# Splitting one block product of each Strassen-like weight product once more, on one core of a Trainium2 chip

## The chip, the cores and the metric

The kernel runs on one NeuronCore of a Trainium2 chip. The metric is the device time of one execution in microseconds (us); less is better. The engines are named as the profile names them: PE is TensorE (PEld its weight loads), DVE is VectorE, ACT is ScalarE, POOL is GpSimd, and SP is SyncE, whose queue starts nearly all of the DMAs.

## The reference, cut to what matters

The input x holds 128 graphs of 128 nodes with 512 features, in float32. Four layers follow one another; each ends with `x = layernorm(x + layer(x))` over the features.

```python
# layer 0
y = einsum('nm,bmd->bnd', adj, x);  out = y @ weight + bias
# layer 1
q, k, v = x @ Wq.T, x @ Wk.T, x @ Wv.T
rel = adjacency.T * (q @ k.T);  rel = rel / norm(rel, axis=2);  out = rel @ v
# layer 2
h = x @ W;  e = leaky_relu(h @ a1 [:, None] + h @ a2 [None, :]) * mask
out = elu(softmax(e) @ h + beta * h)
# layer 3 (W1 = W2 = adj, so C - A is b)
A = einsum('od,bdn->bon', adj, x);  out = max over n of relu(A + b)   # one number per node
```

All products stay in float32. The costly ones are products of a (512 x 512) activation block with a 512 x 512 weight; there are four of them for each set of four graphs.

## The kernel before, in words

**Groups.** The 128 graphs are taken in 32 groups of G = 4, so that a group is a matrix of 512 rows (4 graphs x 128 nodes) by 512 features. Each group passes through `layer0` to `layer3`.

**The four products of a group.** They are called y (weight "0", layer 0), m (weight "m" = Wq and Wk multiplied ahead, layer 1), v (weight "v", layer 1) and z (weight "2", layer 2). Each is a 512 x 512 x 512 product in 2 x 2 blocks of 256, taken in seven block products in place of eight (the scheme of Strassen and Winograd). The sums of the weight's blocks are made once (`weight_blocks`, on DVE). The sums of the left blocks are made for each group on POOL (`left_factors`, four additions of 128x512 for y, for z, and for x, which m and v share; they are the tiles s_y, s_z and s_x). A block product is four matmuls of 128 x 128 weights with 256 columns.

**Where the sums lie.** `product` issues the block products in `ORDER = (1, 2, 6, 5, 7, 3, 4)`. `REGION` says in which PSUM bank each accumulates: 1, 6, 7 and 4 go into one bank (tag r0, which has two buffers), 2 into the bank r12, and 5 and 3 into a later use of r12, which has one buffer. The sums in a bank are used while they grow: after product 1 the bank is read out to output block (0, 0), then product 6 is added on top and the bank is read out to block (0, 1), and so on. So every block product after the first in a bank waits until the read-out before it is done. For m, v and z the first write of an output block (after 1, 6, 5 and 4) is a copy by ACT, and the others are additions by DVE (`out` in `product`). For y all are additions by DVE on top of x, and the two banks are filled with the bias by ACT beforehand (`fill`).

**Order.** Nothing is ordered by data alone. Every operation is emitted with a place in time (`emit(at, f)`), all are sorted by it, and `InOrder` keeps that order on each engine. A place is counted in steps of one block product; a group takes 28 steps, and its four products stand at steps 0 (m), 7 (y of the next group), 14 (v) and 21 (z) of a round. Between the block products stand the other matmuls: `aggregate` (p_y, four matmuls of 128 columns per graph) between those of m, `scores` (p_rel) between those of y, `gather` (p_z) between those of v, and `widen` (p_a) and `attend` (p_o), one matmul of 512 columns per graph, between those of z. Their places are in `TABLE`; the first and last groups have their own in `FIRST` and `LAST`.

**Banks.** PSUM has r0 (2 banks), r12 (1), wa (2) and `bank()` (tag ps, 3), which p_y, p_rel, p_z, p_a and p_o take in turn.

**What stands around the products.** ACT copies p_y to yT and p_z to zT, takes the exponentials (of c into a tile that is also called m, and of e) and the second halves of the layer norms (x from x, nmean, rstd). DVE has the other read-outs, the statistics, `elu` (x from c, x from the exponential m, then the statistics), `dots` (scr from x and wa) and the softmax around `weighted`, which is a POOL multiplication (e from e and adj). `greatest` (nm from e) on DVE waits for it.

Of the kernel before, what the change touches and what calls it, by code (L numbers as in the profile page):

```python
# [8 lines left out]
FP = mybir.dt.float32  # L9
# [20 lines left out]
def kernel(  # L30
# [52 lines left out]
    dram = ctx.enter_context(tc.tile_pool(name="dram", bufs=2, space=bass.MemoryType.DRAM))  # L83

    def bank(name):
        return psum.tile([P, D], FP, tag="ps", name=name, bufs=3)

    def on_all(row, n):

# [27 lines left out]

    w2_sb = const.tile([P, K, D], FP)
    nc.sync.dma_start(w2_sb, w2.rearrange("(k p) f -> p k f", p=P))
    a_sb = data.tile([P, 2, D], FP, tag="x3", name="a_sb")  # L120
    nc.sync.dma_start(a_sb.rearrange("p s d -> p (s d)"), on_all(a2, 2 * D))
    beta_sb = const.tile([P, 1], FP)
    nc.sync.dma_start(beta_sb, on_all(beta, 1))
# [33 lines left out]
    def weight_blocks(at, key, w, keep=0, tag=None):  # L157

        def blk(kh, ch):
            return w[:, 2 * kh : 2 * kh + 2, H * ch : H * ch + H]

        t = {}

        def factor(i):
            if i == 0:
                home, args = (const, {}) if tag is None else (data, dict(tag=tag))
                u = home.tile([P, 3 + keep, 2, H], FP, name=f"t_{key}", **args)
                t.update({2: u[:, 0], 3: u[:, 1], 4: u[:, 2]})  # L170
                t[1] = u[:, 3] if keep else blk(0, 1)
                bw[key] = {
                    1: blk(0, 0), 2: blk(1, 0), 3: blk(1, 1), 4: t[4], 5: t[1], 6: t[2], 7: t[3],
                }
            to, left, op, right = (
                (3, blk(1, 1), ALU.subtract, blk(0, 1)),
                (2, t[3], ALU.add, blk(0, 0)),
                (4, blk(1, 0), ALU.subtract, t[2]),
                (1, blk(0, 1), ALU.subtract, blk(0, 0)),
            )[i]  # L180
            dve.tensor_tensor(t[to], left, right, op)

        for i in range(4):
            emit(at[i], factor, i)

    bw = {}


    def prepare_v(c):
# [7 lines left out]
    def prepare_dots(k):  # L197

        for i in range(2):
            scr = work.tile([P, D], FP, tag="scr", name=f"scr_wa_{i}_{k}", bufs=2)  # L200
            dve.scalar_tensor_tensor(
                scr,
                w2_sb[:, k, :],
                1.0,
                a_sb[:, i, :],
                op0=ALU.mult,
                op1=ALU.mult,
                accum_out=col[:, i, k : k + 1],
            )
# [14 lines left out]
    def emit(at, f, *args):  # L224
        pieces.append((at, lambda: f(*args)))
# [5 lines left out]
    def row(at, step, n=G):  # L231
# [4 lines left out]
        load=[-20], y=row(0.5, 1), y_sums=row(4.3, 0.5), y_w=row(7, 1, 7),  # L236
        stats0=row(14.4, 0.4), norm0=[16.2], apply0=row(16.8, 0.33),
        turn=row(21.4, 1), turn_blocks=row(18.4, 0.6),
        move=row(20.5, 0.1), x_sums=row(25.3, 0.5), m=row(28, 1, 7), scores=row(36.5, 1),
        masked=[39.95], squares=[40.4], turn_rel=[40.3],  # L240
        move_rel=row(41.2, 0.1), inverse=[42.5], v=row(42, 1, 7), attend=row(50.6, 1),
        residual=row(51.0, 1), dots=[51.7, 53.8, 54.9, 55.6], norm1=[54.6], scale=[57.2],
        apply1=row(65.4, 0.33),
        spread=[57.3], leaky=[62.6], weighted=[62.9], greatest=[63.9], exps=[64.0],
        divide=[65.2], turn_att=[68.6], with_beta=[69.0], turn_blocks_2=[65.7], move_2=[65.8], gather=row(71.5, 1),
        z_sums=row(75.3, 0.5), z_w=row(77, 1, 7), exp=[86.0, 87.0, 96.0, 99.6],
        elu=[86.4, 87.4, 96.8, 100.3], norm2=[101.4], apply2=row(102.4, 0.33),
        widen=[104.2, 104.9, 105.6, 106.3], top=[104.7, 105.4, 106.1, 106.8],
# [53 lines left out]
    REGION = {1: 0, 6: 0, 7: 0, 4: 0, 2: 1, 5: 2, 3: 2}  # L302
    BLOCK = {1: (0, 0), 2: (0, 0), 6: (0, 1), 3: (0, 1), 5: (1, 1), 7: (1, 1), 4: (1, 0)}

    def left_factors(at, s, aT, tag, name, keep):
# [14 lines left out]
        emit(at[1], lambda: pool.tensor_tensor(s["f"][6], s["f"][5], blk(0, 0), ALU.subtract))  # L320
        emit(at[2], lambda: pool.tensor_tensor(s["f"][7], blk(0, 0), blk(1, 0), ALU.subtract))
        emit(at[3], lambda: pool.tensor_tensor(s["f"][3], blk(0, 1), s["f"][6], ALU.subtract))

    def by_rows(p, a, b, first):

# [21 lines left out]
                    skip_group_check=True,  # L347
                )

    def product(at, name, mul, s, w, c, fresh, begin=None, before=None, lead=0.7):  # L350
# [29 lines left out]
        def out(i):  # L380
            p, dst = r[REGION[i]], c(*BLOCK[i])
            if fresh and i in (1, 6, 5, 4):
                act.copy(dst, p)
            else:
                dve.tensor_tensor(dst, p, dst, ALU.add)

        for n, i in enumerate(ORDER):
            if before is not None and i in (1, 5):
                emit(at[n] - (0.7 if i == 5 else lead), fill, REGION[i])
            emit(at[n], step, i)  # L390
            emit(at[n] + 0.72, out, i)
# [46 lines left out]
    def layer0(g, t):  # L438
        s = {}

        def aggregate(b):
# [12 lines left out]
                s["yT"][:, :, b * P : (b + 1) * P], p.rearrange("p (k n) -> p k n", k=K)  # L454
            )

        if g > 0:
            emit(t["load"][0], load, g)
        each(t["y"], aggregate)
        left_factors(t["y_sums"], s, "yT", "s_yz", f"y_{g}", 0)  # L460
        product(
            t["y_w"],
            f"y_{g}",
# [4 lines left out]
            False,  # L468
            before=bias_halves,
            lead=4.4 if g == 0 else 0.7,  # L470
        )
        each(t["stats0"], lambda b: stats(s, f"0_{g}", b, x1[g][:, b, :]))
        norm(t["norm0"], t["apply0"], s, f"0_{g}", lambda: x1[g])
# [2 lines left out]
    def layer1(g, t):  # L476
# [128 lines left out]
        def dots(b):  # L605
            if b == 0:
                s["d"] = small.tile([P, 2, G], FP, tag="d12", name=f"d12_{g}")
            for i in range(2):
                scr = work.tile([P, D], FP, tag="scr", name=f"scr_{g}_{b}_{i}", bufs=2)
# [27 lines left out]
        else:  # L637
            each(t["turn_blocks"], turn_blocks)
            each(t["move"], move)
        left_factors(t["x_sums"], s, "xT", "s_x", f"x_{g}", 1)  # L640
        product(t["m"], f"m_{g}", by_columns, s, "m", middle_block, True, begin_middle)
        each(t["scores"], scores)
        emit(t["masked"][0], masked)
        emit(t["squares"][0], squares)
# [3 lines left out]
        else:  # L648
            emit(t["turn_rel"][0], turn_last)
        emit(t["inverse"][0], inverse)  # L650
        product(t["v"], f"v_{g}", by_rows, s, "v", rows_of(lambda: s["v"]), True, begin_values)
        each(t["attend"], attend)
        each(t["residual"], residual)
        if g == NG - 1:
# [10 lines left out]
    def layer2(g, t):  # L665
# [66 lines left out]
            engine.tensor_tensor(e, e, rs[:, :, None].to_broadcast([P, n, P]), ALU.mult)  # L732

        def turn_att(i):
            if i == 0:
                s["p"] = bank(f"p_eT_{g}")
            for b in range(i * n, i * n + n):
                pe.transpose(s["p"][:, b * P : (b + 1) * P], s["e"][:, b, :], ident)

        def with_beta(i):  # L740
            if i == 0:
                s["eT"] = work.tile([P, G, P], FP, tag="eT", name=f"eT_{g}")
            dve.tensor_tensor(
                s["eT"][:, i * n : i * n + n, :],
                s["p"].rearrange("p (b n) -> p b n", b=G)[:, i * n : i * n + n, :],
                beta_b[:, i * n : i * n + n, :],
                ALU.add,
            )
# [57 lines left out]

        def elu(b):
            if b == 0:
                if g < NG - 1:
                    x3[g] = data.tile([P, G, D], FP, tag="x3", name=f"x3_{g}")  # L810
# [21 lines left out]
            emit(t["move_2"][0], move)  # L832
        each(t["gather"], gather)
        if g < NG - 1:
            left_factors(t["z_sums"], s, "zT", "s_yz", f"z_{g}", 0)
            product(t["z_w"], f"z_{g}", by_rows, s, "2", rows_of(lambda: s["c"]), True, begin)
        else:
            each(t["z_w"], direct)
        each(t["exp"], exp)
# [5 lines left out]
    def layer3(g, t):  # L845
        s = {}

        def widen(b):
            s["a", b] = bank(f"p_a_{g}_{b}")
            pe.matmul(s["a", b], adjT, x3[g][:, b, :], start=True, stop=True)  # L850


# [153 lines left out]
```

## Time and profile before

| What | Value |
|---|---|
| Median of 3 runs | 2173.91 us (2173.57 to 2174.77) |
| The profiled execution's own time | 2173.83 us |
| Its span in the profile | 2172.0 us |
| PE matmul busy | 2149.1 us, 99% |
| DVE busy | 1560.6 us, 72% |
| ACT busy | 1115.4 us, 51% |
| POOL busy | 720.8 us, 33% |
| Mean granted PE clock | 0.996 |

The span is the time from the first to the last instruction that the profile shows; the execution's own time has 1.83 us more around it. A matmul in float32 appears as two records. Busy shares are means over the whole span, and matmuls overlap in the records, so the distance from the start of one group of records to the start of the next is the better measure of what a matmul costs PE.

### The profile page before, as it was taken

The numbers are of one execution on the slowest core, as the hardware profiler recorded it, in microseconds if no ns is written. First come the engines' busy times: TensorE is split into PE (matmuls) and PEld (weight loads), VectorE is DVE, ScalarE is ACT, GpSimd is POOL, SyncE is SP. The second block draws the span as 40 slices with busy tenths as digits, with TensorE's granted clock in tenths as the row PEclk, the third lists the DMA queues.
The fourth block names the chain that finished last, engine by engine and source line by source line (L and its number), as shares of the span: only waits on it lengthen the run. The fifth ranks groups of instructions, "written<-read, shape, count | busy, mean of one in ns | idle before, by whom it ended". The sixth has DMA issues, their size and how long they took to land.

```text
span 2172.0 us, 31973 instructions
## 1 busy us (share of the span) xinstructions
PE 2149.1 (99%) x10887; PEld 1820.3 (84%) x10887; DVE 1560.6 (72%) x3429; ACT 1115.4 (51%) x2470; POOL 720.8 (33%) x589
## 2 busy tenths in 40 slices
PE   9999999999999999999999999999999999999996
PEld 8888888888888888888888888888888888888882
DVE  4667676776777776777777767767777767777677
ACT  3235545555545555455555455554455554555554
POOL 4223333333333233334233233323332333333331
PEclk9999999999999999999999999999999999999998
DMA  4012222322122322222222223222322222332201
GB/s 171 25 37 64 58 72 72 71 54 59 59 76 66 77 55 51 67 73 69 55 58 62 74 71 73 54 56 62 75 67 66 58 56 70 74 68 55 39 20 59
DMA packets 361970, 138.31 MB, mean 64 GB/s; under 512 B 303184, under 2 KB 318672, under 8 KB 361808
## 3 DMA queue, kind: packets, MB, share of 16 engines
q1 hardware_dynamic: 361280, 135.22, 24.8%
q8 instruction: 88, 1.44, 0.3%
q10 hardware_dynamic: 528, 1.05, 0.1%
q14 instruction: 74, 0.61, 0.1%
HBM read 55.12 MB, written 41.48 MB: 44 GB/s over the span
## 4 chain that ended last, share of the span: by engine, by line
PE 97%; DVE 2%; ACT 0%; POOL 0%; issue 0%; ACTq 0%; POOLq 0%; DVEq 0%
PE r_m L26 18%; PE r_y L26 18%; PE r_v L26 18%; PE r_z L26 17%; PE p_rel L26 5%; PE p_y L26 5%; PE p_o L26 5%; PE p_z L26 5%; PE p_a L26 5%; PE r_qk L26 1%; DVE st L26 1%; DVE x L26 0%; DVE mx L26 0%; PE first_r L26 0%; ACT x L26 0%; PE c L26 0%
## 5 line engine op out<-in xcount | busy, mean ns | idle before, releaser
L26 ACT ACTIVATE x<-x,nmean,rstd 128x512 f32<-128x512 f32 x384 | 285.4, 807 | 48.6 <-DVE nmean L26 45.1
L26 DVE BATCH_NORM_STATS2 st<-x 128x6 f32<-128x512 f32 x392 | 268.3, 685 | 9.7 <-ACT x L26 1.1
L26 POOL TENSOR_TENSOR rstd<-ve,mhalf 128x4 f32<-128x4 f32 (+1 forms) x99 | 109.3, 1104 | 340.3 <-DVE ve L26 340.3
L26 DVE TENSOR_TENSOR x<-r_y,x 128x512 f32<-128x512 f32 x224 | 152.4, 680 | 91.7 <-PE r_y L26 83.7
L26 ACT COPY yT<-p_y 128x512 f32<-128x512 f32 x128 | 74.9, 586 | 195.6 <-PE p_y L26 195.6
L26 DVE SCALAR_TENSOR_TENSOR scr<-x,wa 128x512 f32<-128x512 f32 x256 | 162.0, 679 | 0.0
L26 DVE TENSOR_REDUCE mx<-p_a 128x1 f32<-128x512 f32 x128 | 88.3, 690 | 99.6 <-PE p_a L26 96.8
L26 ACT ACTIVATE x<-x,mean,r 128x512 f32<-128x512 f32 x128 | 97.4, 808 | 113.9 <-DVE mean L26 112.4
L26 POOL TENSOR_TENSOR rn<-n,mhalf 128x4 f32<-128x4 f32 x32 | 32.6, 1017 | 358.3 <-ACT sq L26 358.3
L26 PEld LDWEIGHTS p_z<-eT,x 128*128 128x128 f32 x1024 | 133.8, 192 | 8.0 <-issue 0.9
L26 PEld LDWEIGHTS p_rel<-xT,tT 128*128 128x128 f32 x1024 | 134.0, 192 | 6.7 <-ACT tT L26 0.2
L26 PEld LDWEIGHTS p_y<-adjT,x 128*128 128x128 f32 x1024 | 133.6, 192 | 6.3
L26 ACT COPY tT<-r_m 128x512 f32<-128x512 f32 x128 | 75.6, 590 | 119.1 <-PE r_m L26 119.1
L26 DVE TENSOR_TENSOR tT<-r_m,tT 128x512 f32<-128x512 f32 x96 | 66.3, 691 | 96.9 <-PE r_m L26 94.2
L26 PE MATMUL p_rel<-xT,tT 128*128 128x128 f32 x1024 | 134.7, 275 | 0.0
L26 PE MATMUL p_z<-eT,x 128*128 128x128 f32 x1024 | 134.5, 275 | 0.1
L26 PE MATMUL p_y<-adjT,x 128*128 128x128 f32 x1024 | 134.1, 275 | 0.0
L26 POOL TENSOR_TENSOR s_y<-yT 128x512 f32<-128x512 f32 x32 | 40.6, 1269 | 281.1 <-ACT yT L26 281.1
L26 PE MATMUL p_a<-x,adjT 128*128 128x512 f32 x256 | 128.7, 606 | 5.1 <-ACT x L26 5.1
L26 ACT COPY zT<-p_z 128x512 f32<-128x512 f32 x128 | 73.7, 576 | 116.5 <-PE p_z L26 116.5
L26 PE MATMUL p_o<-v,relT 128*128 128x512 f32 x256 | 129.7, 592 | 0.0
L26 ACT COPY v<-r_v 128x512 f32<-128x512 f32 x128 | 74.2, 580 | 107.9 <-PE r_v L26 107.9
(157 smaller groups left out, 5218.7 us busy)
## 6 DMA issues: line engine op xcount, KB each, us to landing
out_dram<-x SPq DMA_DIRECT2D x128, 256.0 KB, 2.1
x<-in_x_dram SPq DMA_DIRECT2D x31, 1024.0 KB, 7.6
xT<-xB SPq DMA_DIRECT2D x480, 64.0 KB, 2.3
relT<-relB SPq DMA_DIRECT2D x496, 16.0 KB, 1.8
eBd<-eB SPq DMA_DIRECT2D x30, 256.0 KB, 2.0
eT<-eBd SPq DMA_DIRECT2D x120, 64.0 KB, 2.0
s<-s2d SPq DMA_DIRECT2D x29, 256.0 KB, 5.2
w_sb<-in_L_gnn_weight_dram ACTq DMA_DIRECT2D x1, 1024.0 KB, 6.0
```

The source lines that it names most:

```text
L26: return lambda *args, **kw: self.tc.keep_in_program_order(op(*args, **kw))
```

## The change

One of the seven block products of 256, number 2, is itself taken in seven products of blocks of 128, in place of its four matmuls with 256 columns. It therefore has seven matmuls with 128 columns. Its sums lie in a PSUM bank of their own (tag pi), which is taken from `bank()`: ps has two buffers in place of three. The seven small sums are read out by seven DVE additions of 128x128 onto output block (0, 0), where there was one of 128x512. The left sums of the small product are four POOL additions of 128x128 at the end of `left_factors` (`inner_sums`), and those of the weight are made once on DVE.

The order of a product with a small one inside is `WITH_SMALL`: 1, 6, 5, 7, 3, 4, with the small matmuls in four pieces between them (`SMALL`). `scores` and `gather` stand one step earlier. y of groups 2 to 31, m and v of groups 1 to 30 and z of groups 0 to 29 are taken so: 30 of each, 120 products. Some tiles have fewer buffers (scr, x3, a_sb), and in the last groups some transposes and `widen` use the banks pi and r12.

```diff
     def bank(name):
-        return psum.tile([P, D], FP, tag="ps", name=name, bufs=3)
+        return psum.tile([P, D], FP, tag="ps", name=name, bufs=2)
...
-        move=row(20.5, 0.1), x_sums=row(25.3, 0.5), m=row(28, 1, 7), scores=row(36.5, 1),
+        move=row(20.5, 0.1), x_sums=row(25.3, 0.5), m=row(28, 1, 7), scores=row(35.5, 1),
...
-        divide=[65.2], turn_att=[68.6], with_beta=[69.0], turn_blocks_2=[65.7], move_2=[65.8], gather=row(71.5, 1),
+        divide=[65.2], turn_att=[68.6], with_beta=[69.0], turn_blocks_2=[65.7], move_2=[65.8], gather=row(70.5, 1),
...
+        def inner_sums():
+            a = {
+                (j, k): s[aT][:, 2 + k, j * P : (j + 1) * P] for j in range(2) for k in range(2)
+            }
+            v = work.tile([P, 4, P], FP, tag=tag + "i", name=f"si_{name}")
+            s1, s2, s3, s4 = (v[:, i] for i in range(4))
+            pool.tensor_tensor(s1, a[1, 0], a[1, 1], ALU.add)
+            pool.tensor_tensor(s2, s1, a[0, 0], ALU.subtract)
+            pool.tensor_tensor(s3, a[0, 0], a[1, 0], ALU.subtract)
+            pool.tensor_tensor(s4, a[0, 1], s2, ALU.subtract)
+            s["fi"] = {1: a[0, 0], 2: a[0, 1], 3: s4, 4: a[1, 1], 5: s1, 6: s2, 7: s3}
+
+        if inner:
+            emit(at[3] + 0.01, inner_sums)
...
+    SMALL = (
+        (1.0, (1, 2), 1.3, (((0, 0), 1), ((0, 0), 0))),
+        (2.3, (6, 5), 2.6, (((1, 1), 2), ((0, 1), 0))),
+        (3.3, (7,), 3.8, (((1, 1), 0),)),
+        (4.9, (4, 3), 5.1, (((0, 1), 2), ((1, 0), 0))),
+    )
+    WITH_SMALL = {1: (0.0, 0.72), 6: (1.2, 1.95), 5: (2.4, 3.1), 7: (3.4, 4.3), 3: (5.0, 5.72), 4: (6.0, 6.72)}
+
+    def inner_product(at, name, mul, s, w, c):
+        columns = mul is by_columns
+        q = {}
+        def step(n):
+            if n == 0:
+                q["p"] = psum.tile([P, Q, P], FP, tag="pi", name=f"pi_{name}", bufs=1)
+            for i in SMALL[n][1]:
+                a, b = s["fi"][i], bw_inner[w][i]
+                pe.matmul(
+                    q["p"][:, {2: 1, 5: 2, 3: 2}.get(i, 0), :],
+                    b if columns else a,
+                    a if columns else b,
+                    start=(i == 1),
+                    stop=True,
+                    skip_group_check=True,
+                )
+        def out(n):
+            for (j, h), i in SMALL[n][3]:
+                dst = c(0, 0)
+                x, y = (h, j) if columns else (j, h)
+                dst = dst[:, x, y * P : (y + 1) * P]
+                dve.tensor_tensor(dst, q["p"][:, i, :], dst, ALU.add)
+        for n in range(len(SMALL)):
+            emit(at + SMALL[n][0], step, n)
+            emit(at + SMALL[n][2], out, n)
...
+        if inner:
+            inner_product(at[0], name, mul, s, w, c)
+            for i, (begins, ends) in WITH_SMALL.items():
+                if before is not None and i in (1, 5):
+                    emit(at[0] + begins - lead, fill, REGION[i])
+                emit(at[0] + begins, step, i)
+                emit(at[0] + ends, out, i)
+            return
         for n, i in enumerate(ORDER):
```

More of the change, by code (lines that the diff above doesn't have):

```diff
@@ L119 @@
     nc.sync.dma_start(w2_sb, w2.rearrange("(k p) f -> p k f", p=P))
-    a_sb = data.tile([P, 2, D], FP, tag="x3", name="a_sb")
+    a_sb = data.tile([P, 2, D], FP, tag="x3", name="a_sb", bufs=1)
     nc.sync.dma_start(a_sb.rearrange("p s d -> p (s d)"), on_all(a2, 2 * D))
@@ L181, in factor, with inner @@
             dve.tensor_tensor(t[to], left, right, op)
+        def inner():
+            b = blk(1, 0)
+            quad = {(k, c): b[:, k, c * P : (c + 1) * P] for k in range(2) for c in range(2)}
+            v = const.tile([P, 4, P], FP, name=f"u_{key}")
+            u = {2: v[:, 0], 3: v[:, 1], 4: v[:, 2], 1: v[:, 3]}
+            dve.tensor_tensor(u[3], quad[1, 1], quad[0, 1], ALU.subtract)
+            dve.tensor_tensor(u[2], u[3], quad[0, 0], ALU.add)
+            dve.tensor_tensor(u[4], quad[1, 0], u[2], ALU.subtract)
+            dve.tensor_tensor(u[1], quad[0, 1], quad[0, 0], ALU.subtract)
+            bw_inner[key] = {
+                1: quad[0, 0], 2: quad[1, 0], 3: quad[1, 1], 4: u[4], 5: u[1], 6: u[2], 7: u[3],
+            }
         for i in range(4):
             emit(at[i], factor, i)
-    bw = {}
+        if tag is None:
+            emit(at[3], inner)
+    bw, bw_inner = {}, {}
     def prepare_v(c):
@@ L199, in prepare_dots @@
         for i in range(2):
-            scr = work.tile([P, D], FP, tag="scr", name=f"scr_wa_{i}_{k}", bufs=2)
+            scr = work.tile([P, D], FP, tag="scr", name=f"scr_wa_{i}_{k}")
             dve.scalar_tensor_tensor(
@@ L303, with left_factors @@
     BLOCK = {1: (0, 0), 2: (0, 0), 6: (0, 1), 3: (0, 1), 5: (1, 1), 7: (1, 1), 4: (1, 0)}
-    def left_factors(at, s, aT, tag, name, keep):
+    def left_factors(at, s, aT, tag, name, keep, inner=False):
         def blk(nh, kh):
@@ L322, in left_factors @@
         emit(at[3], lambda: pool.tensor_tensor(s["f"][3], blk(0, 1), s["f"][6], ALU.subtract))
+        def inner_sums():
+            a = {
+                (j, k): s[aT][:, 2 + k, j * P : (j + 1) * P] for j in range(2) for k in range(2)
+            }
+            v = work.tile([P, 4, P], FP, tag=tag + "i", name=f"si_{name}")
[7 more added lines that the diff above has]
+            emit(at[3] + 0.01, inner_sums)
     def by_rows(p, a, b, first):
@@ L348, in by_columns, with product @@
                 )
-    def product(at, name, mul, s, w, c, fresh, begin=None, before=None, lead=0.7):
+    SMALL = (
[30 more added lines that the diff above has]
+            emit(at + SMALL[n][2], out, n)
+    def product(at, name, mul, s, w, c, fresh, begin=None, before=None, lead=0.7, inner=False):
         r = {}
@@ L455, in aggregate @@
             )
+        inner = g >= 2
         if g > 0:
@@ L459, in layer0 @@
         each(t["y"], aggregate)
-        left_factors(t["y_sums"], s, "yT", "s_yz", f"y_{g}", 0)
+        left_factors(t["y_sums"], s, "yT", "s_yz", f"y_{g}", 0, inner)
         product(
@@ L470, in layer0 @@
             lead=4.4 if g == 0 else 0.7,
+            inner=inner,
         )
@@ L608, in dots @@
             for i in range(2):
-                scr = work.tile([P, D], FP, tag="scr", name=f"scr_{g}_{b}_{i}", bufs=2)
+                scr = work.tile([P, D], FP, tag="scr", name=f"scr_{g}_{b}_{i}")
                 dve.scalar_tensor_tensor(
@@ L639, in layer1 @@
             each(t["move"], move)
-        left_factors(t["x_sums"], s, "xT", "s_x", f"x_{g}", 1)
-        product(t["m"], f"m_{g}", by_columns, s, "m", middle_block, True, begin_middle)
+        inner = 1 <= g < NG - 1
+        left_factors(t["x_sums"], s, "xT", "s_x", f"x_{g}", 1, inner)
+        product(
+            t["m"], f"m_{g}", by_columns, s, "m", middle_block, True, begin_middle, inner=inner
+        )
         each(t["scores"], scores)
@@ L650, in layer1 @@
         emit(t["inverse"][0], inverse)
-        product(t["v"], f"v_{g}", by_rows, s, "v", rows_of(lambda: s["v"]), True, begin_values)
+        product(
+            t["v"], f"v_{g}", by_rows, s, "v", rows_of(lambda: s["v"]), True, begin_values,
+            inner=inner,
+        )
         each(t["attend"], attend)
@@ L734, in turn_att @@
         def turn_att(i):
-            if i == 0:
-                s["p"] = bank(f"p_eT_{g}")
+            s["p", i] = psum.tile(
+                [P, D], FP, tag=("pi", "r12")[i % 2], name=f"p_eT_{g}_{i}", bufs=1
+            )
             for b in range(i * n, i * n + n):
-                pe.transpose(s["p"][:, b * P : (b + 1) * P], s["e"][:, b, :], ident)
+                pe.transpose(s["p", i][:, b * P : (b + 1) * P], s["e"][:, b, :], ident)
         def with_beta(i):
@@ L744, in with_beta @@
                 s["eT"][:, i * n : i * n + n, :],
-                s["p"].rearrange("p (b n) -> p b n", b=G)[:, i * n : i * n + n, :],
+                s["p", i].rearrange("p (b n) -> p b n", b=G)[:, i * n : i * n + n, :],
                 beta_b[:, i * n : i * n + n, :],
@@ L808, in elu @@
             if b == 0:
-                if g < NG - 1:
-                    x3[g] = data.tile([P, G, D], FP, tag="x3", name=f"x3_{g}")
+                if g < NG - 2:
+                    x3[g] = data.tile([P, G, D], FP, tag="x3", name=f"x3_{g}", bufs=1)
+                elif g < NG - 1:
+                    x3[g] = work.tile([P, G, D], FP, tag="tv", name=f"x3_{g}")
                 else:
@@ L834, in layer2 @@
         if g < NG - 1:
-            left_factors(t["z_sums"], s, "zT", "s_yz", f"z_{g}", 0)
-            product(t["z_w"], f"z_{g}", by_rows, s, "2", rows_of(lambda: s["c"]), True, begin)
+            left_factors(t["z_sums"], s, "zT", "s_yz", f"z_{g}", 0, not late)
+            product(
+                t["z_w"], f"z_{g}", by_rows, s, "2", rows_of(lambda: s["c"]), True, begin,
+                inner=not late,
+            )
         else:
@@ L848, in widen @@
         def widen(b):
-            s["a", b] = bank(f"p_a_{g}_{b}")
+            other = {
+                (NG - 3, 1): "pi", (NG - 3, 2): "r12", (NG - 2, 0): "pi", (NG - 2, 1): "r12",
+                (NG - 1, 3): "pi", (NG - 2, 3): "r12",
+            }.get((g, b))
+            if other is None:
+                s["a", b] = bank(f"p_a_{g}_{b}")
+            else:
+                s["a", b] = psum.tile([P, D], FP, tag=other, name=f"p_a_{g}_{b}", bufs=1)
             pe.matmul(s["a", b], adjT, x3[g][:, b, :], start=True, stop=True)
```

## The prediction

> **What bounds the kernel now.** I read the page's table of busy shares and its chain of waits first, and ask which engine carries the end.
>
> ```profile
> PE 2149.1 (99%) x10887; PEld 1820.3 (84%) x10887; DVE 1560.6 (72%) x3429; ACT 1115.4 (51%) x2470; POOL 720.8 (33%) x589
> ...
> PE 97%; DVE 2%; ACT 0%; POOL 0%; issue 0%; ACTq 0%; POOLq 0%; DVEq 0%
> ```
>
> PE is never without work. So a shorter stream of matmuls shortens the kernel, and any wait that PE gains lengthens it in full; the other engines count only where PE waits for them. The timeline of PE in one round gives prices, by distances between starts.
>
> ```profile
> 1012.46 1.89 PE L26 MATMUL r_m<-xT,m_qk 128*128 128x256 f32 x8
> 1014.19 1.05 PE L26 MATMUL p_y<-adjT,x 128*128 128x128 f32 x8
> 1015.08 1.89 PE L26 MATMUL r_m<-xT,m_qk 128*128 128x256 f32 x8
> 1016.81 1.05 PE L26 MATMUL p_y<-adjT,x 128*128 128x128 f32 x8
> 1017.70 1.89 PE L26 MATMUL r_m<-s_x,t_m 128*128 128x256 f32 x8
> ...
> 1061.16 1.89 PE L26 MATMUL r_z<-w_sb,zT 128*128 128x256 f32 x8
> ```
>
> A block product takes 1.727 us, four matmuls of 128 columns 0.894 (0.2234 each). The five lines are products 1, 2, 6 of m with p_y between. Product 6 adds onto the bank that product 1 filled, so it waits for ACT's copy of product 1. Now ACT in the same stretch (idle time and its releaser in brackets):
>
> ```profile
> 1015.28 0.58 ACT L26 COPY yT<-p_y 128x512 f32<-128x512 f32 x1 [2.03 <-PE p_y L26]
> 1015.76 0.59 ACT L26 COPY tT<-r_m 128x512 f32<-128x512 f32 x1
> 1017.90 0.58 ACT L26 COPY yT<-p_y 128x512 f32<-128x512 f32 x1 [1.54 <-PE p_y L26]
> 1018.38 0.63 ACT L26 ACTIVATE m<-c 128x512 f32<-128x512 f32 x1
> ...
> 1032.25 0.40 ACT L26 ACTIVATE e<-e,nm 128x128 f32<-128x128 f32 x1 [3.34 <-DVE nm L26]
> ...
> 1033.80 0.57 ACT L26 COPY r_y<-bias_sb 128x512 f32<-128x512 f32 x1
> ...
> 1065.01 0.56 ACT L26 COPY c<-r_z 128x512 f32<-128x512 f32 x1
> ```
>
> ACT takes yT ahead of tT, 0.20 after p_y ends, so product 1 is copied only at 1016.35. Product 6 starts at 1017.70: the wait is hidden with 1.35 us to spare, because product 2 lies between. In z the copy of product 1 ends at 1065.57, 4.41 after the product's start.
>
> ```profile
> 1019.05 0.69 DVE L26 SCALAR_TENSOR_TENSOR x<-m,x 128x512 f32<-128x512 f32 x1 [0.68 <-ACT m L26]
> ...
> 1020.60 0.66 DVE L26 SCALAR_TENSOR_TENSOR x<-c,x 128x512 f32<-128x512 f32 x1
> ...
> 1031.53 0.69 DVE L26 TENSOR_REDUCE nm<-e 128x4 f32<-128x512 f32 x1 [0.73 <-POOL e L26]
> ```
>
> DVE waits at `elu` for ACT's exponential and at nm for POOL's `weighted`:
>
> ```profile
> 1023.80 1.27 POOL L26 TENSOR_TENSOR s_y<-yT 128x512 f32<-128x512 f32 x1 [9.32 <-ACT yT L26]
> ...
> 1030.22 1.28 POOL L26 TENSOR_TENSOR e<-e,adj_sb 128x512 f32<-128x512 f32 x1 [0.63 <-DVE e L26]
> ```
>
> [...]
>
> **The change, part by part.**
>
> *Matmuls.* Each of the 120 products loses 1.727 and gains 7 x 0.2234 = 1.564: 0.163 saved, 0.65 per round of four, 19.5 in all. Bounds: if small matmuls break the stream, they save nothing; with no cost but columns, 0.216 per product, 25.9.
>
> *The cover that goes.* Between 1 and 6 there now lie one piece of the other matmuls and two small matmuls (0.447), not a block product. The instruction order of the changed program still has yT ahead of tT on ACT.
> - m: p_y ends, 0.20 + 0.48 + 0.59 = 1.27 until the copy is done, less 0.45: PE waits 0.82. A restart costs about 0.15 more (near 2109.9 the trace has PE 0.05 after its releaser, and the first nine records 0.24 over their pitch). 0.97.
> - v: `gather`, one step earlier, now puts zT ahead of product 1's copy, as in m: 0.97.
> - z: the copy stands behind the ACT work of layer 3, which isn't moved, and ends at 4.41; product 6 could begin at 1.73 + 0.86 + 0.45 = 3.03. 1.38 + 0.15 = 1.53.
> - y: product 1 is read by DVE, done at about 2.7 against 3.07; nothing.
>
> *The small read-outs.* Small product 7 waits for the read-out of 6, which stands behind `elu` on DVE. In m the exponential now follows yT and the copy of 6: from the end of p_y of graph 1, 0.20 + 0.48 + 0.48 + 0.63 = 1.79, then 0.04, then 1.55 for `elu` (19.05 to 20.60), then two additions 0.21 + 0.29: 3.88. PE has work until 0.45 + 1.73 + 0.89 = 3.07. 0.81 + 0.15 = 0.96. In v the exponential follows zT alone: 3.40 against 3.07: 0.48. In z, DVE is at its densest (`dots`, p_o); its added work there is seven additions at 0.21 to 0.38 apart, 1.6 for 0.6, which lets small pieces 3 and 4 and product 4 wait a little: 0.4, between 0 and 1.2.
>
> *The POOL sums.* `inner_sums` of y stands ahead of `weighted`. y's sums start 0.86 after p_y of graph 3, and that now ends 3.90 before y begins (before: 5.18, as three block products followed). They take 5.79 (1023.80 to 1029.59), the inner four 1.86, `weighted` 1.28: done 5.9 after y's start, not 3.4. nm and, queued behind it on DVE, the first small read-outs end at 7.2; small piece 2 could have begun at 5.69: 1.51 + 0.15. The exponentials of e start 0.72 after nm (1032.25), and the bias fill of r12 behind them ends 2.1 later, at 8.76; product 5 could begin at 7.80: 0.96 + 0.15. Together 2.77; 1.3 if an inner sum takes a quarter of 1.27, 6 if it takes the whole. The inner sums of x and z end 2 us or more before use.
>
> *Edits that I cost at nothing.* ps with two buffers: each tile's last but one has 2.5 us or more of PE work to be read; if that cover goes, one 0.75 read-out per round, 22. `scores` needs only read-outs that end a block product earlier. `gather` starts about 1.7 earlier, at 1045.5; eT has landed by 1043.1. One x3: the stores land by 1079.4, the next `elu` writes at 1083.7. scr is DVE's alone. SP's issues keep their order. Weight sums: 16 additions, 4.6 us, in DVE's idle time; at most 1.2 for the four ahead of the first y. First and last groups: 0, plus or minus 3.
>
> *Sum per round.* 0.97 + 0.96 + 0.97 + 0.48 + 1.53 + 0.40 + 2.77 = 8.08, less 0.65 = 7.43; 30 rounds: 223. With the profiled execution's own 2173.83 (span 2172.0, 1.83 around it; the median is 2173.91) that is **2397 us**. Each wait is counted from where PE itself stood last, so an earlier wait doesn't shorten the next.
>
> **The rivals.**
> - *Faster: the matmul stream alone counts.* If the waits add up to less than the 0.65 that a round saves, the time is down to 2154. For it: PE's 97% of the chain, and 28% idle DVE. Against it: ACT's order, which puts 0.82 on PE in m alone.
> - *Only the bank waits.* If POOL and DVE keep up, as their idle shares suggest, what remains is product 6 in m, v and z: 3.47 - 0.65 = 2.82 per round, 85: 2258.
> - *POOL's small sums cost as much as big ones*, 1.27 each: 3.2 more per round in y: 2494. [...]
> - *Not what it says.* The instruction order shows seven matmuls per small product and one r12 use less, so this falls.
>
> **How the numbers follow.** My sum and its neighbourhood 0.66; only bank waits 0.22; dear POOL sums 0.05; faster 0.05; the two cancelling 0.02. The range, 2245 to 2480, takes in the bank waits alone and, above, 2.8 more per round. About 0.2% (4 us) is what a measurement can tell from no change: faster 0.05, same 0.02, slower 0.93.
>
> **What would show it.** PE's busy time falls towards 2130 and its share to about 89%. The waits should show PE idle for product 6: r_m and r_v about 0.8 us each behind ACT's tT and v, r_z 1.4 behind c; pi_m about 0.8 behind DVE's read-out; pi_y and r_y behind DVE and ACT's bias fill. If PE doesn't wait in front of product 6, or the four-matmul groups of pi are not at 0.22 per matmul, the forecast is wrong at its root; if POOL's inner sums are done before `weighted` is due, its y term is.

## The result, and the profile after

The changed kernel takes **2449.24 us** (median of 4 runs, 2447.97 to 2449.83) against 2173.97 of the kernel before on the same chip (2173.57 to 2174.77): the ratio is 1.1265, interval 1.1245 to 1.1284. It is slower by 275 us, where 223 were forecast. The profiled execution took 2447.97, of which 2445.9 are span. In this document "the kernel after" is the changed kernel.

The busy shares and the chain of waits on the page of the kernel after:

```profile
PE 2228.2 (91%) x11607; PEld 1870.0 (76%) x11607; DVE 1685.8 (69%) x4165; ACT 1115.2 (46%) x2470; POOL 885.2 (36%) x949
...
PE 61%; ACT 15%; POOL 12%; DVE 11%; issue 2%; ACTq 0%; DVEq 0%; POOLq 0%
```

PE was 97% of the chain and is now 61%. ACT, POOL and DVE have taken 38% between them, although none of them is anywhere near full. PE's busy time is *up* by 79 us, not down by 19.5; that will need an explanation. The PE part of the table of waits (engine, tile, what ended the wait: us in total, times, longest):

```profile
PE pi_y L26 <- DVE x L26: 51.1, 30, 1.7
PE r_z L26 <- ACT c L26: 39.7, 29, 1.4
PE r_y L26 <- ACT r_y L26: 26.2, 31, 0.9
PE pi_m L26 <- DVE tT L26: 22.0, 29, 0.8
PE r_v L26 <- ACT v L26: 21.5, 30, 0.7
PE r_m L26 <- ACT tT L26: 21.1, 26, 0.9
PE pi_v L26 <- DVE v L26: 5.2, 29, 0.2
```

Each comes some 30 times, once in a round. They are the waits of the forecast, one by one. Product 6 of m, in the timeline of PE and ACT:

```profile
1142.24 0.61 PE L26 MATMUL pi_m<-xT,m_qk 128*128 128x128 f32 x4
1142.44 0.59 ACT L26 COPY yT<-p_y 128x512 f32<-128x512 f32 x1 [2.03 <-PE p_y L26]
1142.92 0.59 ACT L26 COPY tT<-r_m 128x512 f32<-128x512 f32 x1
1143.66 1.97 PE L26 MATMUL r_m<-s_x,t_m 128*128 128x256 f32 x8 [0.81 <-POOL si_x L26]
```

pi_m is the only work left between product 1 and product 6, and it ends, at 0.2234 from the start of one matmul to the start of the next, 0.45 after its own start, at 1142.69. ACT takes yT first and is done with tT at 1143.51; PE goes on at 1143.66. The releaser named here is POOL's si_x, because an addition of POOL also ended at 1143.66; product 6 does not read that tile, in 26 of the rounds the same wait is put down to ACT's tT, and in all of them PE goes on 0.14 after the end of ACT's copy. The copy of product 1 of z and the product 6 behind it:

```profile
1124.59 0.56 ACT L26 COPY c<-r_z 128x512 f32<-128x512 f32 x1
...
1125.30 1.97 PE L26 MATMUL r_z<-t,s_z 128*128 128x256 f32 x8 [1.37 <-ACT c L26]
```

And the y stretch, POOL, DVE, ACT and PE together, in the timeline:

```profile
1160.33 0.45 POOL L26 TENSOR_TENSOR si_y<-yT 128x128 f32<-128x128 f32 x1
...
1161.68 0.46 POOL L26 TENSOR_TENSOR si_y<-yT,si_y 128x128 f32<-128x128 f32 x1
...
1162.09 1.27 POOL L26 TENSOR_TENSOR e<-e,adj_sb 128x512 f32<-128x512 f32 x1
1163.40 0.69 DVE L26 TENSOR_REDUCE nm<-e 128x4 f32<-128x512 f32 x1 [3.54 <-POOL e L26]
1164.00 0.61 DVE L26 TENSOR_TENSOR x<-pi_y,x 128x128 f32<-128x128 f32 x2
...
1164.75 0.68 PE L26 MATMUL pi_y<-u,si_y 128*128 128x128 f32 x4 [1.74 <-DVE x L26]
...
1165.67 0.57 ACT L26 COPY r_y<-bias_sb 128x512 f32<-128x512 f32 x1
...
1166.30 3.42 PE L26 MATMUL r_y<-w_sb,s_y 128*128 128x256 f32 x8 [0.86 <-ACT r_y L26]
...
1169.55 1.05 PE L26 MATMUL p_rel<-xT,tT 128*128 128x128 f32 x8
```

Read it downward: four small sums on POOL, then the weighting, then nm, then the small read-outs that stand behind nm on DVE, then PE's second small piece; the exponentials behind nm on ACT, then the bias fill, then PE's product 5. The last two lines hold what nobody forecast: product 5 takes 3.25 us from start to start, where a block product takes 1.73. The same stretches by window, with the granted clock of PE:

```profile
core 0: us, PE busy (x) PEld busy (x) DVE busy (x) ACT busy (x) POOL busy (x), PEclk, DMA share, GB/s
1162.85:1166.30 3.45, 0.85 (x7) 0.53 (x5) 2.24 (x7) 2.13 (x9) 0.51 (x1) 0.93 0.00 0
1166.30:1169.55 3.25, 3.25 (x8) 2.64 (x9) 1.94 (x8) 2.29 (x4) 0.00 (x0) 0.55 0.14 54
1169.55:1177.19 7.64, 7.64 (x48) 7.02 (x46) 4.98 (x13) 2.43 (x10) 1.02 (x1) 1.00 0.17 50
```

PE has 0.85 us of work in the 3.45 us ahead of product 5, and then its clock is granted at 0.55. The product runs at about half speed, is counted as busy all that time, and the clock is back afterwards. Over the run this adds some 50 us of busy time. The rest of the extra comes of the waits: each shows the tail of the group ahead of it (0.61 busy for a group whose pitch is 0.45) and a slower first matmul (0.07 to 0.10), 0.24 by seven by 30, again some 50 us; less the 19.5 saved that makes the 79.

### The profile page after: what moved, and what is told of

Same layout as the page of the kernel before. It is cut to its first block, busy times and chain, and to the rows that moved or that the text cites. A ratio compares the mean times of both kernels' runs of the same rounds, so it can differ in the third digit from the quotient of the medians.

```text
span 2445.9 us, 34309 instructions
## 1 busy us (share of the span) xinstructions
PE 2228.2 (91%) x11607; PEld 1870.0 (76%) x11607; DVE 1685.8 (69%) x4165; ACT 1115.2 (46%) x2470; POOL 885.2 (36%) x949
## 3 DMA queue, kind: packets, MB, share of 16 engines
q8 instruction: 93, 1.52, 0.3%
## 4 chain that ended last, share of the span: by engine, by line
PE 61%; ACT 15%; POOL 12%; DVE 11%; issue 2%; ACTq 0%; DVEq 0%; POOLq 0%
PE r_v L26 12%; PE r_y L26 11%; PE r_z L26 10%; PE r_m L26 7%; POOL s_y L26 5%; PE p_o L26 4%; PE p_z L26 3%; PE p_y L26 3%; DVE st L26 3%; PE p_rel L26 3%; DVE x L26 3%; POOL yT L26 2%; ACT x L26 2%; PE p_a L26 2%; POOL si_y L26 2%; ACT yT L26 2%
## 5 line engine op out<-in xcount | busy, mean ns | idle before, releaser
L26 DVE TENSOR_TENSOR x<-r_y,x 128x512 f32<-128x512 f32 x194 | 132.7, 684 | 111.1 <-PE r_y L26 107.6
L26 PE MATMUL r_y<-w_sb,s_y 128*128 128x256 f32 x512 | 164.4, 478 | 25.9 <-ACT r_y L26 25.9
L26 DVE SCALAR_TENSOR_TENSOR scr<-x,wa 128x512 f32<-128x512 f32 x256 | 174.8, 683 | 5.7
L26 PEld LDWEIGHTS r_y<-w_sb,s_y 128*128 128x128 f32 x512 | 120.3, 246 | 52.0 <-ACT r_y L26 31.6
L26 PE MATMUL r_z<-t,s_z 128*128 128x256 f32 x496 | 119.7, 384 | 41.7 <-ACT c L26 39.7
L26 DVE SCALAR_TENSOR_TENSOR x<-m,x 128x512 f32<-128x512 f32 x128 | 88.6, 692 | 94.9 <-ACT m L26 88.2
L26 PE MATMUL r_m<-s_x,t_m 128*128 128x256 f32 x512 | 123.3, 384 | 24.3 <-ACT tT L26 21.1
L26 PE MATMUL r_v<-t_v,s_x 128*128 128x256 f32 x512 | 124.2, 385 | 21.5 <-ACT v L26 21.5
L26 ACT ACTIVATE e<-e,nm 128x128 f32<-128x128 f32 x128 | 49.8, 390 | 186.9 <-DVE nm L26 186.9
```

What stands on the lines that cost most here:

```text
L26: return lambda *args, **kw: self.tc.keep_in_program_order(op(*args, **kw))
```

## The experiments

The **theory** was the forecast's: the time is the sum of waits that PE meets because two things that used to hide read-outs are gone or displaced, and each can be taken away alone by changing one place in an engine's order. A **second theory** was added on seeing the windows: two of these waits, close together, are followed by half clock on PE. The **rival** to both was that the small matmuls, the banks or the extra work of DVE and POOL cost the time themselves, so that changes of order bring little.

### One wait at a time

**e1**: the read-out of product 1 stands at 0.45 in place of 0.72, ahead of yT and zT on ACT.

```diff
-    WITH_SMALL = {1: (0.0, 0.72), 6: (1.2, 1.95), 5: (2.4, 3.1), 7: (3.4, 4.3), 3: (5.0, 5.72), 4: (6.0, 6.72)}
+    WITH_SMALL = {1: (0.0, 0.45), 6: (1.2, 1.95), 5: (2.4, 3.1), 7: (3.4, 4.3), 3: (5.0, 5.72), 4: (6.0, 6.72)}
```

> Product 1 is read out at place 0.45 in place of 0.72, so that ACT copies it ahead of yT in m, ahead of zT in v, and one layer-3 graph earlier in z. Nothing else is changed. Theory (PE waits for product 1's copy, in order on ACT): the waits in front of product 6, 1.04 us in m, 0.98 in v and 1.60 in z, go; in m some 0.5 us come back, because the first small read-outs stand behind dots on DVE: about 3.1 us in each of 30 rounds, 94 us, so about 2355 us (2340 to 2370). Rival (DVE or POOL is the bound now, and PE only waits where it happens to): the time comes back at the next wait, and the kernel stays above 2420 us.

Measured: 2349.71 us, ratio 1.0806 (1.0772 to 1.0839). The waits of r_m and r_v are gone, as they should be. That of r_z was to go too and falls only from 39.7 to 22.3; pi_m's stays (19.3). That the total still came out as expected is in part luck: product 5 of y was slowed in 12 rounds only, against 28 in the kernel after; the 16 rounds by 1.52 make some 24 us. For m and v it is shown that ACT's order made the waits for product 6; in z half of the wait went, and the rest goes in e5, where the read-out stands at 0.35. The run also gave evidence on the clock that was not planned. From the timeline of PE in e1, two rounds:

```profile
835.25 0.68 PE L26 MATMUL pi_y<-u,si_y 128*128 128x128 f32 x4 [1.47 <-DVE x L26]
836.79 3.64 PE L26 MATMUL r_y<-w_sb,s_y 128*128 128x256 f32 x8 [0.86 <-ACT r_y L26]
...
907.94 0.68 PE L26 MATMUL pi_y<-u,si_y 128*128 128x128 f32 x4 [1.46 <-DVE x L26]
909.49 1.99 PE L26 MATMUL r_y<-w_sb,s_y 128*128 128x256 f32 x8 [0.86 <-ACT r_y L26]
```

The same two waits come in both rounds, 1.47 and 0.86, yet one product 5 is slowed and the other not. Of the 18 rounds between 250 and 1500 us, 14 had waits of 1.44 to 1.48 and 0.86, and 7 of these were slowed; four had 0.69 and 0.86, and none was.

**e2**: POOL's small sums of y stand behind the weighting.

```diff
-            emit(at[3] + 0.01, inner_sums)
+            emit(at[3] + (1.2 if aT == "yT" else 0.01), inner_sums)
```

> The four small POOL sums of y stand behind weighted in place of ahead of it. Nothing else is changed. Theory: nm comes 1.9 us earlier, the wait of 1.9 us in front of small piece 2 of y goes, and of the wait for the bias fill about 0.9 us stay; that is 1.9 to 2.2 us in 30 rounds, 57 to 66 us: about 2387 us. If the halved PE clock in product 5 of y is an answer to the 3 us without matmuls ahead of it, it goes too, 1.5 us more: about 2341 us. Rival (the clock dip belongs to the matmuls, or to chance): product 5 still takes 3.25 us, and the time is about 2387 us.

Measured: 2355.21, ratio 1.0831 (1.0799 to 1.0862), 94 us less than after. The wait of pi_y is gone; the fill's is left, and product 5 at full speed:

```profile
1122.48 1.99 PE L26 MATMUL r_y<-w_sb,s_y 128*128 128x256 f32 x8 [0.86 <-ACT r_y L26]
```

**e3**: the bias fill for product 5 is issued at 0.75 after y's start, ahead of the exponentials on ACT, in place of 0.7 ahead of the product.

```diff
-                    emit(at[0] + begins - lead, fill, REGION[i])
+                    emit(at[0] + (0.75 if i == 5 else begins - lead), fill, REGION[i])
```

> ACT fills the bank r12 with the bias ahead of the exponentials of y's round in place of behind them. Nothing else is changed. Theory: the 1.0 to 1.1 us in front of product 5 of y go, the 1.9 us in front of small piece 2 stay: 30 to 33 us, about 2417 us. If the clock dip needs both waits together, it goes as well and the time is about 2372 us; if one wait of 1.9 us is enough for it, product 5 keeps its 3.25 us.

Measured: 2372.01, ratio 1.0908 (1.0877 to 1.094), 77 us less, of which the wait itself (26.2) and its restarts are about 33. The timeline shows the rest:

```profile
1129.87 0.68 PE L26 MATMUL pi_y<-u,si_y 128*128 128x128 f32 x4 [1.75 <-DVE x L26]
1130.39 1.89 PE L26 MATMUL r_y<-w_sb,s_y 128*128 128x256 f32 x8
```

A wait of 1.75 alone left the clock whole here (no record of products 5 and 3 of y is longer than 382 ns, where the kernel after has up to 796), and so did the 0.86 alone in e2 (up to 483). In these runs the slow product 5 came only with both waits, and taking away either brought its 1.52 us back.

**e4**: e2 and e3 together.

> Both of the two edits for y: small POOL sums behind weighted, and the bias fill ahead of the exponentials. Theory: y loses both waits and the clock dip, 1.9 + 1.1 + 1.5 = 4.5 us in 30 rounds, 135 us: about 2314 us (2300 to 2330). Rival (the clock dip stays without the waits): about 2360 us.

Measured: 2321.79, ratio 1.0677 (1.0646 to 1.0708), 127.5 less than after. Alone, e2 and e3 brought 94.0 and 77.2, in sum 171.2. The 43.7 between are the clock, which both had counted: 28 slowed rounds by 1.52 are 42.6. No wait is left in y.

**e6**: the read-out of the second small piece comes 0.32 step sooner, ahead of `elu` on DVE.

```diff
-        (2.3, (6, 5), 2.6, (((1, 1), 2), ((0, 1), 0))),
+        (2.25, (6, 5), 2.28, (((1, 1), 2), ((0, 1), 0))),
```

> The changed kernel with one edit: the second pair of small read-outs ahead of elu on DVE. Theory: the waits of 1.0 us in m and 0.44 us in v in front of small product 7 go, 1.4 us in 30 rounds, 43 us: about 2406 us. Rival (ACT's exponential, which elu waits for, then holds DVE later and PE waits somewhere else): 2430 to 2450 us.

Measured: 2371.10, ratio 1.0904 (1.0882 to 1.0926), 78 less where 43 were expected. The waits of pi_m fall from 22.0 to 6.0 and pi_v's are gone. The remainder I had not foreseen: in y the wait of 1.74 splits into 0.36 ahead of product 6 and 0.68 ahead of the second piece, and with 0.68 and 0.86 the clock stayed whole (the records of products 5 and 3 of y, which share one row of the page, take 385 ns in mean; 478 after).

### All orders at once

**e5**: e1 (with 0.35 in place of 0.45), e2, e3 and e6 together.

> All order edits together: product 1 read out at place 0.35, y's small POOL sums behind weighted, the early bias fill, and the second pair of small read-outs at place 2.28 (its matmuls at 2.25), which puts it ahead of elu on DVE in m and v. The split itself is unchanged. Theory (the matmul saving of 0.65 us per round is real and was buried under waits that come from order alone): what stays is some 0.8 us in m, where the first small read-outs stand behind dots, and up to 0.5 us in z: 2154 + 30 x 1.0 to 1.3, about 2189 us (2175 to 2205). Rival (the added work of DVE and POOL costs time whatever its order): above 2250 us.

Measured: 2214.68, ratio 1.0186 (1.0171 to 1.0201): 234.6 of the 275 us are gone by four places in the order, but some 26 more than expected stays, 10 above the range. The table of waits shows where:

```profile
PE pi_m L26 <- DVE tT L26: 22.0, 58, 0.8
PE r_y L26 <- DVE x L26: 10.3, 29, 0.4
```

Once m starts sooner behind z, its small read-outs meet `dots` of the group before on DVE (the larger part of pi_m, two waits per round now); and product 6 of y waits for the read-out of y's product 1.

**e7**: the rest of the change without the split. No product is taken in seven small ones; the two banks of ps, the earlier `scores` and `gather` and the fewer buffers stay.

```diff
-        inner = g >= 2
+        inner = False
...
-        inner = 1 <= g < NG - 1
+        inner = False
```

> The changed kernel without the split itself: product 2 is taken whole everywhere and in the old order, and what stays of the change is two banks for ps, single x3, a_sb and scr, the earlier places of scores and gather, and the borrowed banks in the last groups. Theory (these cost nothing in the steady rounds): 2174 us within 6 us. Rival (two banks are too few, and part of the loss is theirs): 2190 us or more.

Measured: 2182.98, ratio 1.0039 (1.0024 to 1.0054): 8.4 more than before, where at most 6 was allowed for. So the edits that I costed at nothing cost 8 us in all. A round is 66.22 us in place of 66.05 (from v's start to the next, over 27 rounds) and the opening is some 3 us longer; which of the edits does it was not tried.

**e8**: e5 with `dots` and what hangs on it later.

```diff
-        residual=row(51.0, 1), dots=[51.7, 53.8, 54.9, 55.6], norm1=[54.6], scale=[57.2],
+        residual=row(51.0, 1), dots=[51.7, 53.8, 54.9, 57.35], norm1=[54.6], scale=[57.4],
...
-        spread=[57.3], leaky=[62.6], weighted=[62.9], greatest=[63.9], exps=[64.0],
+        spread=[57.45], leaky=[62.6], weighted=[62.9], greatest=[63.9], exps=[64.0],
```

> All order edits together, and besides the last of the four dots of a group, with the scaling and the DMA behind it, stands behind the first small read-outs of m. Theory: of the wait in front of m's small piece 2 (about 0.8 us) nearly all goes, 20 to 25 us below the kernel with all order edits: about 2167 us (2155 to 2185), at or a little below the kernel before. Rival (DVE is the bound there and elu takes the wait over): no gain on the kernel with all order edits.

Measured: 2193.23, ratio 1.0085 (1.0068 to 1.0101). pi_m's wait falls from 22.0 to 6.0, as meant, but the time misses the range by 8. DVE, POOL and PE around y's start:

```profile
1105.87 1.26 POOL L26 TENSOR_TENSOR yT<-yT 128x512 f32<-128x512 f32 x1
1105.89 2.12 DVE L26 TENSOR_TENSOR e<-s,d 128x512 f32<-128x512 f32 x1
...
1107.10 1.99 POOL L26 TENSOR_TENSOR s_y<-yT,s_y 128x512 f32<-128x512 f32 x1
1108.04 1.59 DVE L26 SCALAR_TENSOR_TENSOR e<-e 128x512 f32<-128x512 f32 x1
1109.56 0.68 DVE L26 TENSOR_TENSOR x<-r_y,x 128x512 f32<-128x512 f32 x1
...
1110.38 1.97 PE L26 MATMUL r_y<-t,s_y 128*128 128x256 f32 x8 [0.34 <-DVE x L26]
```

The addition for e takes 2.12 us, where other DVE additions of that size take 0.69, while POOL's big sums run beside it (the last section has more of these times). y's read-out stands behind it, and PE waits 0.34.

### The last waits

**e9**: e8 with DVE's addition for e and the leaky step earlier, ahead of the read-out of m's product 3, and the third small read-out ahead of `elu`.

```diff
-        spread=[57.45], leaky=[62.6], weighted=[62.9], greatest=[63.9], exps=[64.0],
+        spread=[57.45], leaky=[61.15], weighted=[62.9], greatest=[63.9], exps=[64.0],
...
-                dots=row(57.8, 0.1), scale=[58.9], spread=[61.6]),
+                dots=row(57.8, 0.1), scale=[58.9], spread=[61.6], leaky=[62.6]),
...
-        (3.3, (7,), 3.8, (((1, 1), 0),)),
+        (3.3, (7,), 3.35, (((1, 1), 0),)),
```

> e8 with two read-outs of DVE brought forward: the small products' third read-out ahead of the second elu row (at 3.35 in place of 3.8), and DVE's addition for e with the leaky step after it (2.12 and 1.59 us in e8, beside POOL's sums) ahead of the read-out of m's product 3 rather than behind it. What e8 still loses per round is 0.34 us ahead of product 6 of y, 0.21 ahead of the last small piece of m, and about 0.4 us of restarts and of the late last piece. THEORY (the waits left are only a matter of what stands ahead of a read-out on DVE): e add 1104.0 to 1106.1 on e8's clock, leaky to 1107.7, m's read-out to 1108.4, just ahead of the relation scores that need it (1108.5), y's first read-out to 1109.4 where product 6 asks at 1110.0; both waits go, about 2193 - 30*0.65 = 2173, range 2163 to 2180, not below before by more than 0.5%. RIVAL: the addition beside two POOL sums takes longer still and the relation scores now wait for m's read-out by 0.3 us or more: 2185 to 2200.

Measured: **2163.76 us** (2163.11 to 2164.55), ratio **0.9952** (0.9938 to 0.9965): faster than the kernel before by 10.6 us, or 0.5%, and than e8 by 29.5, at the lower end of the range. The two waits of e8 (16.2 in sum) went, and with each of their 58 occurrences the tail and the slower start, 0.24, which I had counted only in part. The page, and DVE and PE at y's start:

```profile
PE 2130.7 (99%) x11607; PEld 1827.8 (85%) x11607; DVE 1672.9 (77%) x4165; ACT 1121.1 (52%) x2470; POOL 871.1 (40%) x949
```

```profile
1092.57 0.69 DVE L26 TENSOR_TENSOR x<-r_y,x 128x512 f32<-128x512 f32 x1 [0.69 <-ACT r_y L26]
1093.19 0.61 PE L26 MATMUL pi_y<-w_sb,yT 128*128 128x128 f32 x4
...
1093.63 1.89 PE L26 MATMUL r_y<-t,s_y 128*128 128x256 f32 x8
```

y's read-out ends at 1093.26 and product 6 starts at 1093.63 with no wait. No wait is left that comes in every round; PE is busy 99%, with 2130.7 us. No run has this order without the split, but the order alone had nothing to win from the kernel before: PE's waits there sum to some 9 us, each comes at most three times, and none recurs from round to round.

**e10**: e8 with the third read-out as in e9, and in place of moving the leaky step as a whole, its maximum alone behind y's first read-out. In doing so the weighting was placed at 63.45.

```diff
+            s["e"] = e
+
+        def leaky_rest():
+            e = s["e"]
             dve.scalar_tensor_tensor(e, e, ALPHA, e, op0=ALU.mult, op1=ALU.max)
-            s["e"] = e
...
         emit(t["leaky"][0], leaky)
+        emit(t["leaky"][0] + (0.8 if 0 < g < NG - 2 else 0.0), leaky_rest)
...
-        spread=[57.45], leaky=[62.6], weighted=[62.9], greatest=[63.9], exps=[64.0],
+        spread=[57.45], leaky=[62.6], weighted=[63.45], greatest=[63.9], exps=[64.0],
```

> e8 with the same earlier third read-out (3.35 in place of 3.8), and, in place of moving the whole leaky step, only its second half moved: the addition for e stays, y's first read-out comes next on DVE, then the leaky maximum, and POOL's weighting after it. THEORY: the read-out of y's product 1 ends 0.5 us ahead of product 6, the wait of 0.34 goes with the one of 0.21, about 2173, range 2163 to 2180; the maximum ends about 0.5 us later than in e8, so weighting and nm come later by as much, which no matmul of that stretch waits for. RIVAL: nm, later by 0.5 us, puts off the small read-outs of y behind it and the second piece of y waits again by 0.3 us or so: 2183 to 2195.

Measured: 2220.35, ratio 1.0212 (1.0198 to 1.0226), a miss by 47. The wait of product 6 is gone, but one line has come back:

```profile
PE pi_y L26 <- DVE x L26: 50.4, 30, 1.7
```

That is the wait of the kernel after. At 63.45 the weighting had fallen behind the small sums of y, which stand at 63.0.

**e11**: e10 with the small sums at 1.7 behind the big ones, so again behind the weighting; nothing else.

> e10 with one place changed: y's small POOL sums stand at 1.7 after the big ones in place of 1.2. In e10 the weighting had been put at 63.45 and so fell behind the small sums at 63.0, the order of the kernel after, and PE waited 50.4 us in 30 rounds for pi_y. THEORY (that order alone is what e10 lost against e9, 56.6 us): the waits of 1.74 go, about 2164, as e9; range 2160 to 2176, the upper part if the read-outs behind nm, which here comes 0.5 us later than in e9, still keep the second small piece by up to 0.3 us. RIVAL: e10's loss came of splitting the leaky step, and the wait stays: 2205 to 2220.

Measured: 2175.37, ratio 1.0002 (0.9993 to 1.001), 45.0 less than e10 by one place in POOL's order. What is left against e9 is this:

```profile
PE pi_y L26 <- POOL si_y L26: 5.8, 29, 0.3
```

The weighting starts later here, so the small sums behind it come 0.2 too late for the second piece. The upper part of the range was right, the releaser was another than I had named.

**e12**: e9 with the first group's `dots` later, against a single wait of 2.43 us in the first round.

```diff
-                dots=row(57.8, 0.1), scale=[58.9], spread=[61.6], leaky=[62.6]),
+                dots=row(58.3, 0.1), scale=[58.9], spread=[61.6], leaky=[62.6]),
```

> e9 with the dot products of the first group on DVE at 58.3 in place of 57.8, behind the read-out of the small products' second piece, because e9's one long wait of PE outside the last groups is 2.43 us, once, in front of m's small product 7 of the first round, behind DVE's d. THEORY: that wait goes and nothing else moves: 2163.8 - 2.4 = 2161.3, range 2160.5 to 2162.5. RIVAL: the dot products are then late for the transposes p_s that read d, 5 us further on, and the wait comes back there: 2163 to 2165.

Measured: 2167.69, ratio 0.9968 (0.9955 to 0.998), 3.9 more than e9, which ran on another chip: a miss, neither the theory nor the rival. The dots now stand ahead of the third small read-out, and the wait there is 3.58 us. The windows of that wait and of the product behind it:

```profile
105.25:109.50 4.25, 0.67 (x6) 0.52 (x5) 4.11 (x9) 1.08 (x2) 3.32 (x3) 1.00 0.00 0
109.55:112.95 3.40, 3.40 (x11) 2.57 (x10) 0.49 (x2) 0.00 (x0) 1.61 (x2) 0.51 0.00 0
```

One wait of 3.58 us came here by itself: the clock is 0.51 for the next 3.40 us, and one block product takes 3.56 us, about twice its time. In e9 the wait of 2.43, a piece earlier in the same product, was followed by a block product at full speed (1.89); the same wait of 2.43 in e8 was followed by half clock (2.63), and the last section has the work in the windows of both. The longer wait (1.15) and the clock (1.67) make 2.8 of the 3.9; where the rest lies was not found.

## Why the prediction was right, and where its size was off

The direction, the cause and the place of nearly all the time were right: PE's stream did get shorter, and seven waits outweighed it. Term by term, per round, forecast and then measured in the kernel after (from where PE's own work ended to its next start, with the slower first matmuls behind it, 0.07 to 0.10):

| Term | Forecast | Measured |
|---|---|---|
| Product 6 of m, of v, behind ACT's copy | 0.97, 0.97 | 1.04, 0.98 |
| Product 6 of z | 1.53 | 1.60 |
| Small product 7 of m, of v, behind `elu` | 0.96, 0.48 | 1.00, 0.44 |
| The rest in z | 0.40 | 0.21 |
| Second small piece of y, behind nm | 1.66 | 1.90 |
| Product 5 of y, behind the bias fill | 1.11 | 1.1 |
| Product 5 of y itself, at half clock (28 rounds) | not in the sum | 1.52 |
| Sum | 8.08 | 9.79 |
| Less the matmuls saved | 0.65 | 0.65 |

9.14 by 30 is 274; as product 5 was slowed in 28 of the 30 rounds, it is 271, where the change measured 275. The distance from v's start in one round to the next says the same: 75.13 us (23 rounds from 275.19 to 2003.24) against 66.05 before (27 rounds from 251.02 to 2034.43).

**The matmul saving** was right at its price (four small matmuls 0.45 apart, 0.2234 each) and is seen alone in e9: PE is busy 2130.7, near the 2130 forecast. That e9 is 10.6 faster, and not 19.5, is the 8.4 of e7, which lies in the edits I had costed at nothing. That nothing was too low by 8 us. The account closes: 2174.3 - 19.5 + 8.4 = 2163.2 for a kernel with the change and none of its waits; e9 has 2163.76.

**The cover that goes.** e1 shows it for product 6 of m and v and e6 for the small read-outs: the waits vanish, or shrink to 0.2 for pi_m, when the read-out is moved ahead in its own engine's queue, with no work removed.

**The POOL sums.** The forecast's 1.86 us for the four small sums were not shown by the trace of before, which has no POOL sum of that size; the kernel after has 0.45 to 0.46 for each and 1.81 for the four of y (1160.33 to 1162.14). The 0.29 for a small read-out stands in the trace of before, where an addition of the same size, e<-e,rs, takes 292 ns; the small read-outs took 274 to 284. e2 and the pair e10 and e11 show that it is their place ahead of the weighting that costs: 94 us, the clock included, and 45 us for one position.

**The step that was mis-sized** is the sum itself: it took a wait to cost its length and a restart of 0.15. In y two waits, 1.9 and 1.1 with 0.45 of work between, cost 1.52 more in 28 rounds, 43 us in all, four fifths of the 52 by which the forecast was low; the term for PE's clock was left out. The sum's range reached 2.8 per round above it and so took this in, but none of that was set aside for the clock: that is luck. PE's share (91%, not 89) and its busy time (2228, not 2130) are off by the slowed product and by the longer records around each wait, about half each. The profile of before had the sign of it, in the last group, and the forecast made no use of it: the windows of the kernel before over the four p_a records behind waits of 1.14 and 3.17 us.

```profile
2148.98:2152.40 3.42, 3.35 (x4) 0.80 (x4) 3.21 (x11) 3.42 (x6) 0.21 (x1) 0.61 0.20 77
```

**The rivals.** "Only the bank waits" fell: e1 removed most of these, and the kernel was still at 1.08. "POOL's sums as dear as big ones" fell with 0.46. "Faster: the stream alone counts" was false for this order of work, but e9 is what it described, 10 us above its 2154: the same computation, with the order set so that no wait recurs.

## What to carry to other kernels

When PE is full, matmuls that are taken out may have been the cover of a read-out: for each bank that is read while it grows, add up what PE has to do between the write and the next write, and compare it with the queue of the engine that reads it. The waits here were priced by the place of one instruction in its engine's order, so look first at what stands ahead of it and try that place; here seven such places turned 275 us lost into 10.6 gained. Add up neighbouring waits of PE too: in the kernel after, the windows of 3.41 us in which they left it without work for 1.86 us or more were followed by half clock.

## What the runs showed of the hardware that I had not expected

**PE's clock stood at half after windows of 3.41 us in which PE had been busy for at most 45.4% (the kernel after), also where several short waits made up the rest.** Waits of 0.68 and 0.86 close together (e6) and of 1.75 alone (e3) left it whole. 1.47 and 0.86 were followed by half clock in 7 rounds of 14 (e1); 1.74 and 0.86 in 28 rounds of 29 (the kernel after; in the round at 1241.86 product 5 took 1.83). A single 2.43 was followed by it in e8 and not in e9; a single 3.58 was (e12). In the trace of the kernel after, the granted clock stands at 0.50 in 30 stretches, and all of them start on one grid of 3.413 us: the 28 in its rounds last 3.41 us each, the two of the last groups 6.83 and 12.64. With that grid laid over the trace, 30 of the 683 windows at full clock were followed by half clock, and PE was busy for at most 45.4% of each; in the 653 others it was busy for at least 49.1%. The kernel before has two stretches at 0.50, both in the last groups; PE was busy for at most 22.6% of the windows ahead of them, and for at least 51.0% of the 629 others. The two rounds of e1 shown above, by such windows:

```profile
833.34:836.75 3.41, 1.12 (x8) 0.77 (x7) 2.19 (x6) 2.13 (x9) 0.52 (x1) 1.00 0.02 5
836.76:840.17 3.41, 3.38 (x8) 2.76 (x9) 1.97 (x8) 2.42 (x4) 0.00 (x0) 0.50 0.16 65
905.02:908.43 3.41, 1.95 (x15) 1.74 (x13) 1.77 (x4) 1.12 (x6) 1.53 (x2) 1.00 0.00 0
908.44:911.85 3.41, 2.55 (x15) 2.16 (x14) 2.67 (x10) 2.40 (x7) 0.00 (x0) 1.00 0.00 0
```

In the first round both waits fall into one window, which has 1.12 us of work, and the next is at half clock; in the second they are divided between two windows, with 1.95 and 2.55. The wait of 2.43 left 1.31 us of work in its window in e8, and the block product behind it took 2.63; in e9, where it was divided between two windows, it left 1.66, and the product took 1.89. In the kernel after, the starts of the slow stretches in its rounds lie 75.09 us apart, 22 windows (once 44), so nearly every round met the grid in the same way.

**DVE's work on e took longer beside POOL's sums, and they beside it.** The addition for e took 2.12 us beside the big sums in e8, 1.76 in the round of e9 and 1.36 in one of e10, with the same operands, and POOL's sums 1.26 to 1.99. In e8 the addition ended 0.88 after the POOL sum that had begun just ahead of it, and POOL's next sum took 1.99, about one such addition (0.69) more than its 1.27. In the kernel after, DVE's leaky step on e (e<-e, 128x512) took 1.56 to 1.60 us in the 30 groups in which a POOL instruction ran beside it and 0.69 in the two in which none did; the read-outs of y (x<-r_y,x) took 0.65 to 0.69 with one beside them and without. So the time of the addition for e was not a constant of it, and a place in the order that hid it in one of these kernels did not hide it in the next.
